# Cross-attention kernel: one unit of a batch's value projections moved from the fourth stretch of its half to the third

## The chip, the cores and the metric

The kernel runs on one core of a Trainium2 chip. The metric is the device time of one execution in microseconds; before the change the median of 3 runs is 1578.23 us (1575.32 to 1578.86).

## The reference, cut to what matters

`x` has 32 batches of 64 rows by 256; the context has 1601 rows by 256 for each batch. Three layers follow each other; the change lies in the first, cross-attention with 16 heads of 16.

```python
qh = _split_heads(q @ wq_w.T + wq_b)          # q = layernorm(x)
kh = _split_heads(k @ wk_w.T + wk_b)          # k = v = context
vh = _split_heads(v @ wv_w.T + wv_b)          # the values' projection
scores = jnp.einsum('bhqd,bhkd->bhqk', qh, kh) / jnp.sqrt(jnp.float32(D_K))
scores = jnp.where(mask, scores, jnp.float32(-1000000000.0))
attn = jax.nn.softmax(scores, axis=-1)
out = jnp.einsum('bhqk,bhkd->bhqd', attn, vh)
```

A second layer (a span attention, with `W_span`, `W_val`, `W_out`) works on the 64 rows of each batch, a third is a mixture of experts. All is float32.

## The kernel before, in words

**Halves.** The first layer goes through 64 halves, `n` = 0 to 63: half `n` is batch `b` = n // 2 and `c` = n % 2, eight of the sixteen heads. The context's 1601 rows are cut into 13 blocks of 124 (the last has 113), in four groups `GROUPS` of 4, 3, 3 and 3 blocks. Work is pipelined: in half `n` the scores of half `n + 1` are made, the exponentials of half `n`, the products with the values of half `n - 1`, and the projections of batch `b + 1`.

**Stretches.** A half runs through four stretches, `g` = 0 to 3, one for each group. In stretch `g`:

- `scores(n + 1, g, ...)`: PE multiplies queries and keys into four banks of PSUM (`psc`, L495), DVE adds the mask and puts them into `prob` (L504), and takes running maxima (`maximum`, L525). The last running maximum writes `mx`.
- `project_keys` for batch `b + 1`: PE makes `pk` (L450 by way of `product`), ACT copies it with its bias into `kT` (L465). In stretch 3 it is tiled.
- `project_values(b + 1, u, tiled)`: one unit `u` is two blocks of 124 rows (unit 6 has one), PE makes `pv` (L450), ACT copies it into `v` (L482). Untiled, a block takes two matmuls of 124 output rows; tiled, each is cut into four of 32 (the last of 28), at their own columns of the array. The profile counts two instructions for each float32 matmul, so a unit is 8 matmul instructions untiled and 32 tiled, each with a load of its weights.
- `less_maxima` on POOL (L556), an `exponentials` on ACT (L561), and one step of what the agenda holds for this stretch (`run`): steps of the queries of the next two batches (`query_steps`) and of the second layer for a pair of batches (`span_steps`), with work on all engines, such as `po` (L218, PE).

In stretch 0 the maxima of half `n` are also turned: `pm` (L532, PE) waits for `mx`, DVE reduces it to `mc` (L539), `pb` (L547, PE) spreads it, ACT copies it to `mb` (L551), and POOL takes it off. The products with the values, `values(n - 1, r)` (`pvs`, L571), stand in two parts: one ahead of stretch 0, one at its end.

**Order and banks.** PE, DVE, ACT and POOL run in the order in which the program is written (`manual_schedule`). All of `psc`, `pk`, `pv`, `pm`, `pb`, `po` and their like share the six banks of `ps_x`; a product waits until the bank that it is given has been read out.

**Where the units stand.** For batch `b + 1`, the first half (`c` = 0) makes unit 0 in stretch 1 and units 1 and 2, tiled, in stretch 3; the second half makes unit 3 in stretch 1, unit 4 in stretch 2, units 5 and 6, tiled, in stretch 3. Stretch 2 of a first half has none.

## Time and profile before

| | |
|---|---|
| median of 3 runs | 1578.23 us (1575.32 to 1578.86) |
| the profiled execution | 1579.34 us, its span 1577.4 us |
| mean granted clock of TensorE | 0.995 |
| `pv` untiled, 128*124 128x256 | 792 matmul instructions |
| `pv` tiled, 128*32 and 128*28 128x256 | 2604 and 744 matmul instructions |
| PE matmul and weight-load instructions | 28600 and 28600 |
| PE waits: `psc` L495 for DVE `prob` L504 (from 40 to 1390 us) | 20.9 us, 43 times |
| PE waits: `pm` L532 for DVE `mx` L525 (from 40 to 1390 us) | 4.6 us, 14 times |

The span is the time from the first instruction to the last. A line of a timeline gives the start of a run of like instructions, how long it lasts, the engine, the line of the kernel, the operation, output and inputs with their sizes (for PE rows*columns of the weights and the moving block), how many there are, and in brackets the idle time of the engine before it and what ended it. Ends of matmuls are modelled, so runs overlap their followers by some tenths of a microsecond, and start to start is the better measure. A line of the windows view gives a window's bounds and length, the busy time and count of PE, PEld, DVE, ACT and POOL, then the granted clock of TensorE, the DMA share and GB/s.

### The profile page before, as it was taken

Reading aid. Unit: us, or ns where it says so; the run is one execution under the profiler, and the core shown is the slowest. Engines: PE = TensorE matmul, PEld = TensorE weight load, DVE = VectorE, ACT = ScalarE, POOL = GpSimd, SP = SyncE. Lnnn points to the kernel's source line nnn. Section 1 sums busy time; section 2 is a strip of 40 time slices with the busy share of each in tenths; the row PEclk is TensorE's granted clock in tenths of the full one; section 3 lists DMA queues with packets and bytes.
Section 4 is the critical chain, followed back from the end, with each engine's and each line's share of the span. In section 5 each row is a group of like instructions: output and inputs, shape, how many; then the busy total and the mean of one; then the engine's idle time right before and its main releaser. Section 6 shows DMA issues by size and latency. Waiting matters only on the chain.

```text
span 1577.4 us, 62735 instructions
## 1 busy us (share of the span) xinstructions
PE 1518.3 (96%) x28600; PEld 1090.8 (69%) x28600; DVE 1259.5 (80%) x2700; ACT 897.1 (57%) x1229; POOL 1121.6 (71%) x424
## 2 busy tenths in 40 slices
PE   8999999999999999999999999999999999988899
PEld 5676776777767676676767676676767676754587
DVE  4888889898888888898889988898888988884200
ACT  2565656566565656656666656565655656555311
POOL 1777877878687877788786977788786878761610
PEclk9999999999999999999999999999999999999999
DMA  5111111111111111111111111111111111004100
GB/s 166 54 42 44 36 38 38 45 51 44 51 44 44 39 41 35 35 51 44 52 44 51 36 43 38 38 38 45 51 44 52 44 37 41 7 2 154 57 27 27
DMA packets 52072, 73.78 MB, mean 47 GB/s; under 512 B 3812, under 2 KB 51040, under 8 KB 51680
## 3 DMA queue, kind: packets, MB, share of 16 engines
q1 hardware_dynamic: 50992, 69.00, 15.3%
q8 instruction: 224, 3.67, 1.0%
q10 hardware_dynamic: 816, 0.79, 0.2%
q14 instruction: 40, 0.33, 0.1%
HBM read 65.57 MB, written 4.19 MB: 44 GB/s over the span
## 4 chain that ended last, share of the span: by engine, by line
PE 60%; DVE 36%; issue 2%; ACT 1%; DMA 1%; POOL 1%; ACTq 0%; SPq 0%; DVEq 0%; POOLq 0%
DVE prob L504 14%; PE pv L450 13%; PE pk L450 13%; DVE mrun L525 12%; PE pvs L571 9%; PE psc L495 9%; PE py L853 4%; PE u L600 3%; PE pm L532 2%; PE ph L835 2%; PE pb L547 1%; DVE total L313 1%; DVE least L308 1%; DVE mrun L293 1%; PE po L343 1%
## 5 line engine op out<-in xcount | busy, mean ns | idle before, releaser
L556 POOL TENSOR_TENSOR prob<-prob,mb 124x1664 f32<-124x1664 f32 x252 | 936.6, 3735 | 275.2 <-ACT mb L551 188.2
L504 DVE TENSOR_TENSOR prob<-psc,madd 124x384 f32<-124x384 f32 (+1 forms) x1024 | 567.5, 580 | 152.2 <-PE psc L495 152.2
L525 DVE TENSOR_TENSOR mrun<-prob,mrun 124x512 f32<-124x512 f32 x704 | 483.5, 687 | 3.9
L561 ACT ACTIVATE prob<-prob 124x1664 f32<-124x1664 f32 x256 | 403.1, 1587 | 26.0 <-POOL prob L556 23.0
L450 PE MATMUL pk<-ct,wkT_sb 128*32 128x361 f32 (+2 forms) x1768 | 404.8, 499 | 9.5 <-DMA wkT_sb<-in_wkT 5.4
L450 PE MATMUL pv<-wvT_sb,ct 128*32 128x256 f32 (+3 forms) x4268 | 385.8, 379 | 0.0
L450 PEld LDWEIGHTS pv<-wvT_sb,ct 128*32 128x32 f32 (+3 forms) x4268 | 258.6, 123 | 128.8 <-issue 16.3
L495 PE MATMUL psc<-qbd,kT 32*124 32x128 f32 x6656 | 288.2, 285 | 24.1 <-DVE prob L504 21.5
L465 ACT ACTIVATE kT<-pk,cols 128x372 f32<-128x372 f32 (+2 forms) x256 | 152.1, 594 | 239.4 <-PE pk L450 239.1
L495 PEld LDWEIGHTS psc<-qbd,kT 32*124 32x124 f32 x6656 | 226.2, 181 | 89.3 <-DVE prob L504 47.0
L482 ACT COPY v<-pv 124x512 f32<-124x512 f32 (+1 forms) x224 | 124.9, 558 | 211.0 <-PE pv L450 210.8
L450 PEld LDWEIGHTS pk<-ct,wkT_sb 128*32 128x32 f32 (+1 forms) x1768 | 158.6, 145 | 119.3 <-issue 51.5
L571 PE MATMUL pvs<-prob,v 124*17 124x64 f32 x13312 | 213.2, 220 | 2.3 <-issue 2.2
L571 PEld LDWEIGHTS pvs<-prob,v 124*17 124x17 f32 x13312 | 195.8, 98 | 22.5 <-issue 13.8
L517 ACT COPY mrun<-prob 124x512 f32<-124x512 f32 x64 | 38.5, 602 | 59.5 <-DVE soft L295 56.3
L855 DVE SCALAR_TENSOR_TENSOR ot<-py,prob 128x256 f32<-128x256 f32 x16 | 6.8, 425 | 75.7 <-PE py L853 66.1
L600 PE MATMUL u<-xfT,sw_sb 128*128 128x512 f32 x128 | 60.2, 620 | 1.3 <-ACT vbd L262 0.9
L547 PEld LDWEIGHTS pb<-cst,mc 128*124 128x124 f32 x256 | 29.2, 136 | 36.5 <-DVE mc L539 29.4
L532 PE MATMUL pm<-cst,mx 124*128 124x124 f32 x256 | 40.7, 282 | 8.3 <-DVE mx L525 8.2
L525 DVE TENSOR_TENSOR mx<-prob,mrun 124x512 f32<-124x512 f32 x64 | 43.9, 686 | 2.2
L842 ACT ACTIVATE hT<-ph,cols 128x256 f32<-128x256 f32 x32 | 13.4, 471 | 56.3 <-PE ph L835 56.3
L600 PEld LDWEIGHTS u<-xfT,sw_sb 128*128 128x128 f32 x128 | 24.5, 198 | 29.9 <-issue 25.3
(126 smaller groups left out, 1143.4 us busy)
## 6 DMA issues: line engine op xcount, KB each, us to landing
ct<-in_ctxT SPq DMA_DIRECT2D x64, 372.0 KB, 3.2
ct<-in_ctxT SPq DMA_DIRECT2D x32, 496.0 KB, 3.6
ct<-in_ctxT SPq DMA_DIRECT2D x32, 361.0 KB, 3.1
w<-in_w SPq DMA_DIRECT2D x16, 256.0 KB, 5.9
x<-in_x SPq DMA_DIRECT2D x16, 128.0 KB, 2.2
x_kept<-x SPq DMA_DIRECT2D x16, 128.0 KB, 2.8
prob<-x_kept SPq DMA_DIRECT2D x8, 256.0 KB, 5.4
out<-ot SPq DMA_DIRECT2D x16, 128.0 KB, 1.9
```

Of the source, the lines that this page charges most:

```text
L450: nc.tensor.matmul(out[at:end], lhsT=lhsT[:, at:end], rhs=rhs, start=start, stop=stop, **(dict(tile_position=(0, at)) if tiled else {}),)
L465: nc.scalar.activation(kTs[c][:, k0 : k0 + kn], ps[:, :kn], AF.Identity, bias=cols[:, B_K + c : B_K + c + 1])
L482: nc.scalar.copy(vs[b % 2][:kn, 2 * u : 2 * u + n, :, :DK], ps[:kn, : n * D].rearrange("p (n h d) -> p n h d", n=n, d=DK),)
L495: nc.tensor.matmul(ps[:CHUNK, k * P : (k + 1) * P], lhsT=kTs[c][32 * j : 32 * j + 32, at : at + CHUNK], rhs=qbd[b // 2][32 * j : 32 * j + ...
L504: nc.vector.tensor_tensor(pair_of(n, j)[:, c0 : c0 + nb, :].rearrange("p k (e q) -> p k e q", e=2), ps[:CHUNK, : nb * P].rearrange("p (k e ...
L525: nc.vector.tensor_tensor(dst, block_of(n, k), run, ALU.max)
L532: nc.tensor.transpose(ps[:, j * CHUNK : (j + 1) * CHUNK], m[:CHUNK, j, :], ident[:CHUNK, :CHUNK])
L556: engine.tensor_tensor(sj, sj, m[:CHUNK, j, None, :].to_broadcast([CHUNK, NKC, P]), ALU.subtract)
L561: nc.scalar.activation(pair_of(n, j), pair_of(n, j), AF.Exp)
L571: nc.tensor.matmul(pvs[32 * j : 32 * j + DK + 1, c, :, r, :], lhsT=v[:kn, k, 8 * c + h, :], rhs=pair_of(n, h // 2)[:kn, k, (h % 2) * S : ( ...
L600: nc.tensor.matmul(ps, lhsT=w[:, c, hc * P : (hc + 1) * P], rhs=xfT[:, c, :, slot], start=(c == 0), stop=(c == 1),)
L853: nc.tensor.matmul(py, lhsT=x, rhs=w, start=(n == 0), stop=(n == len(terms) - 1))
```

## The change

Unit 1 moves from stretch 3 to stretch 2 of a first half, and is no longer tiled. Stretch 3 of a first half keeps unit 2, tiled. Second halves are as they were. The loop makes batch `b + 1` in 31 first halves (`b` = 0 to 30); the units of batch 0 are made ahead of it and are not touched.

```diff
                 project(project_keys, c, g, g == 3)
                 if g == 1:
                     project(project_values, 3 * c)
-                elif g == 2 and c:
-                    project(project_values, 4)
-                elif g == 3:
-                    for u in range(5 if c else 1, 7 if c else 3):
+                elif g == 2:
+                    project(project_values, 3 * c + 1)
+                else:
+                    for u in (5, 6) if c else (2,):
                         project(project_values, u, True)
             if g:
                 less_maxima(n, g, m, nc.gpsimd)
```

On PE's queue the unit's matmuls now stand between the keys of stretch 2 and the agenda's step and scores that follow; on ACT's queue its copy stands ahead of the agenda's step and the exponential of stretch 2. No other engine's queue and no DMA changes its order.

## The prediction

> **What bounds the kernel now.** I read the page's busy shares and chain of waits first, then the timelines of PE and DVE over four halves in mid run, and last the busy time and granted clock of short windows.

> ```profile
> PE 1518.3 (96%) x28600; PEld 1090.8 (69%) x28600; DVE 1259.5 (80%) x2700; ACT 897.1 (57%) x1229; POOL 1121.6 (71%) x424
> PE 60%; DVE 36%; issue 2%; ACT 1%; DMA 1%; POOL 1%; ACTq 0%; SPq 0%; DVEq 0%; POOLq 0%
> ```

> PE and DVE take turns on the chain. I take the starts of pm (L532), one a half, as milestones. A half's usual length depends on its place in a cycle of two batches: A (even batch, first half) 21.96 us, B (even, second) 22.22, C (odd, first) 23.05, D (odd, second) 19.91; together 87.14. The change touches A and C. This is PE in one C (batch 13, from 601.53), from the keys of stretch 2 on:

> ```profile
> 612.99 1.52 PE L450 MATMUL pk<-ct,wkT_sb 128*128 128x372 f32 x4
> 614.44 0.97 PE L495 MATMUL psc<-qbd,kT 32*124 32x128 f32 x6
> 616.00 0.92 PE L495 MATMUL psc<-qbd,kT 32*124 32x128 f32 x18 [0.59 <-DVE prob L504]
> 616.84 1.42 PE L450 MATMUL pk<-ct,wkT_sb 128*32 128x361 f32 x16
> 618.08 3.64 PE L450 MATMUL pv<-wvT_sb,ct 128*32 128x256 f32 x64
> 621.53 1.64 PE L571 MATMUL pvs<-prob,v 124*17 124x64 f32 x104
> 623.10 1.15 PE L495 MATMUL psc<-qbd,kT 32*124 32x128 f32 x32
> 624.58 0.61 PE L532 MATMUL pm<-cst,mx 124*128 124x124 f32 x4 [0.33 <-DVE mx L525]
> ```

> The scores of stretch 3 stand from 614.44 to 616.84, 2.40 us for what takes 0.86 elsewhere (632.85 to 633.71): 1.54 us lost on a bank that DVE has not emptied. DVE is busy all through C and ends it:

> ```profile
> 617.52 1.01 DVE L504 TENSOR_TENSOR prob<-psc,madd 124x384 f32<-124x384 f32 x2
> 623.75 0.69 DVE L525 TENSOR_TENSOR mx<-prob,mrun 124x512 f32<-124x512 f32 x1
> ```

> mx ends at 624.44 and pm starts 0.14 us later. A is alike, with the scores at 569.00 to 570.85 (0.99 lost) and mx ending at 578.49:

> ```profile
> 569.00 0.48 PE L495 MATMUL psc<-qbd,kT 32*124 32x128 f32 x4
> 569.78 0.92 PE L495 MATMUL psc<-qbd,kT 32*124 32x128 f32 x20 [0.30 <-DVE prob L504]
> 577.55 1.15 PE L495 MATMUL psc<-qbd,kT 32*124 32x128 f32 x32
> 578.64 0.64 PE L532 MATMUL pm<-cst,mx 124*128 124x124 f32 x4
> ```

> So in A and C the end is DVE's. B and the start of D are PE's: in D, DVE stands 2.35 us until PE has done pm, pk, pb, pvs and the scores of stretch 1 (624.58 to 629.74).

> **The moved unit itself.** In 31 first halves unit 1 leaves stretch 3 and enters stretch 2. Tiled it cost half of 618.08 to 621.53, 1.73 us. Untiled, keys then unit then scores take 1.36 + 1.81 (633.71, 635.07, 636.88, in a D) against 1.45 for keys then scores (612.99 to 614.44): 1.72. Net 0.0. Each half issues 24 matmuls and 24 weight loads fewer; no DMA, POOL or SP work moves.

> **Is DVE made late?** In C the unit runs 614.35 to 616.17, while the scores would have waited. They start at 616.17, and D shows 0.95 from such a start to DVE's first read (628.81 to 629.76): 617.12, and DVE wants them at 617.52, so 0.4 us of cover. In A: unit, then po (0.96), scores at 570.73, readable at 571.68; wanted at 572.57. Cover 0.9. Banks: the unit takes the free bank, so the scores use those of stretch 2, as in D, where 24 scores run unbroken and only the tiled keys wait, 0.14. Without the cover: if the fourth score waited for DVE's last read of stretch 2 (616.46 + 0.54 = 617.00), 18 more instructions at 0.84 would end at 617.84 and DVE start near 618.0, 0.46 later in each of 14 C. That is the upper bound; below nothing it can't go, DVE being busy throughout.

> **ACT.** The unit's copy (L482) now stands ahead of L304 and L561 and waits for its matmuls (1.92 from their start, as 608.23 to 610.15): in C 616.27 instead of never. Behind it, the square ends near 617.8 (POOL wants it at 618.70) and the exponential near 619.3 (PE's pvs wants it at 620.0, being early itself). Nobody waits; 0.

> **Where PE's won time goes.** In C PE reaches the scores before pm at 616.17 + 0.86 + 1.24 + 1.73 + 1.57 = 621.57 and is done at 622.72. mx still ends at 624.44. So the losses of stretch 3 become one wait of **1.86 us** at pm. In A it is 0.9. Neither A nor C gets shorter. Three small gains:
> - Batches 0 and 1 are not DVE's at the end of their first half (pm 0.75 and 0.74 after mx, not 0.14): 0.6 each, 1.2.
> - PE's instruction supply. Queue q8 brings 3.67 MB in 224 packets, so 16.4 KB or 256 of PE's 57,200 instructions each, and PE sometimes stands until the next:

> ```profile
> q8 instruction: 224, 3.67, 1.0%
> 650.26 0.30 PE L571 MATMUL pvs<-prob,v 113*17 113x64 f32 x6 [0.62 <-issue]
> ```

> Nine A are longer than usual, by 4.75 us in all, and eight B, by 3.25. In four A (batches 8, 10, 20, 22) it falls in the last scores, 2.5 us: now inside the 0.9 us of wait. In B 2.8 of it falls soon after pm: packets asked for earlier, while PE waits at pm, come in time. All D, which follow a wait of 0.33 at pm, are 19.91 to 19.92 from batch 3 on. The early stalls of A (2.3) stay. Gain 5.3; bounds 0 and 8, as the 48 instructions shift where packets end.
> Sum: -1.2 - 5.3, about **-6 us**.

> **What the wait does to the clock.** This decides. Late in the run PE has gaps, and the granted clock falls to half for whole windows of 3.41 us on a fixed grid:

> ```profile
> 1389.46:1392.87 3.41, 1.88 (x40) 1.38 (x36) 2.79 (x6) 1.60 (x2) 0.00 (x0) 1.00 0.00 0
> 1427.01:1430.42 3.41, 1.38 (x100) 1.21 (x88) 3.20 (x8) 2.38 (x3) 1.89 (x1) 1.00 0.29 75
> 1430.42:1433.83 3.41, 3.34 (x12) 2.78 (x12) 0.65 (x2) 1.17 (x2) 0.02 (x1) 0.50 0.73 233
> 1464.55:1467.97 3.42, 1.60 (x29) 1.21 (x33) 0.66 (x1) 1.21 (x3) 1.47 (x1) 1.00 0.00 0
> ```

> The third number is PE's busy time, PEclk the third from the end. A window with 1.38 us busy (a gap of 2.10) is followed by 0.50, and so is 1.60; 1.88 is not (a gap of 1.53). The new gap, whole inside a window, leaves 3.41 - 1.86 = 1.55 busy: below one that fell. Cost: at half clock 104 pvs took 2.98 us (1416.20) against 1.64, so a window loses 3.41 / 2 = **1.7 us**, just after C's pm, where D is PE's and nothing hides it.

> How often: the window needs at least 3.41 - 1.60 = 1.81 of the gap. That holds for (3.41 + 1.86 - 3.62) / 3.41 = 48% of positions. A cycle of 87.14 is 25.53 windows, so after a kept C the next gap lies half a window on; with 1.7 lost it is 88.84, 26.03 windows, and the next falls again until leftover stalls carry it out. I estimate 11 of the 14 C from batch 3 on: **+18.7 us**. Bounds: 0 (threshold under 1.55 busy) and 14 x 1.7 = 24. I take near the upper one, as 1.55 is nearer to 1.60, which fell, than to 1.88. A's 0.9 us gap leaves 2.5 busy, above 1.88: no fall.

> [...]

> **Sum.** -6 + 18.7 = +12.7. On the profiled execution's 1579.34 (span 1577.4) that is 1592.0; it stands 1.1 over the median 1578.23, so **1591** as a median.

> **Rivals.** (1) The clock holds, as the threshold lies lower or the gap comes out under 1.6: only -6, 1572 (1569 to 1575). For: every C loses 1.54 us in one place today and keeps 1.00. Against: the 1.60 window. (2) It holds and supply stalls merely move: -1.2 or so, 1577 (1575 to 1581). (3) The scores starve DVE: the bank case above, 14 x 0.46 = +6.4, and -1.2: 1583. It decides once the scores are over 0.4 us late. Against: D's unbroken scores.

> **Chances.** Forecast 0.54, its own range 1584 to 1597; rivals 0.28, 0.12, 0.06. Range 1571 to 1596. A measurement here tells 0.2%, 3.2 us: faster 0.28, same 0.12, slower 0.54 + 0.06 = 0.60.

> **What would show it.** PE's wait at pm for mx grows to near 1.9 us in C and 0.9 in A, and the scores' waits for DVE fall from 20.9 us to near 9 (those of stretch 2). Windows after C's pm stand at 0.50 and D grows to 21.6; the mean clock falls from 0.995 to near 0.983. If D stays 19.91, the clock step is wrong; if C grows past 23.05, the cover of DVE is.

## The result, and the profile after

After the change a run takes 1578.22 us (median of 20, 1570.56 to 1588.58), before it 1578.84 (20 runs, 1575.32 to 1583.53). The ratio is 0.9996, with an interval from 0.9982 to 1.001: no change that can be told. The forecast was 1591. The profiled execution after took 1575.67 us, its span 1573.6.

PE's line, the chain and the instruction queue on the page of after:

```profile
PE 1499.1 (95%) x27856; PEld 1094.7 (70%) x27856; DVE 1258.5 (80%) x2700; ACT 895.6 (57%) x1229; POOL 1121.5 (71%) x424
PE 55%; DVE 41%; issue 2%; ACT 1%; POOL 1%; DMA 0%; DVEq 0%; ACTq 0%; POOLq 0%
q8 instruction: 218, 3.57, 0.9%
```

PE has 744 matmuls and as many weight loads fewer, which is 24 in each of 31 first halves. PE's share of the chain has gone from 60% to 55%, DVE's from 36% to 41%. This is PE in the same C (batch 13) as in the prediction, from the keys of stretch 2 on:

```profile
610.05 1.52 PE L450 MATMUL pk<-ct,wkT_sb 128*128 128x372 f32 x4
611.40 1.89 PE L450 MATMUL pv<-wvT_sb,ct 128*124 128x256 f32 x8
613.22 0.93 PE L495 MATMUL psc<-qbd,kT 32*124 32x128 f32 x24
614.12 1.42 PE L450 MATMUL pk<-ct,wkT_sb 128*32 128x361 f32 x16
615.36 1.91 PE L450 MATMUL pv<-wvT_sb,ct 128*32 128x256 f32 x32
617.09 1.64 PE L571 MATMUL pvs<-prob,v 124*17 124x64 f32 x104
618.65 1.15 PE L495 MATMUL psc<-qbd,kT 32*124 32x128 f32 x32
621.55 0.64 PE L532 MATMUL pm<-cst,mx 124*128 124x124 f32 x4 [1.74 <-DVE mx L525]
```

The scores of stretch 3 run unbroken (613.22 to 614.12, where it was 2.40 us), and all that PE won stands as one wait of 1.74 us at pm. PE's waits from 40 to 1390 us, in total, times and longest:

```profile
PE pm L532 <- DVE mx L525: 34.4, 28, 1.7
PE psc L495 <- DVE prob L504: 7.9, 14, 0.6
```

Before, these were 4.6 us in 14 and 20.9 us in 43. The wait has changed its place, as the prediction said. The halves from batch 3 on, 14 of each kind, summed from start of pm to start of pm:

| | before, us | after, us | usual one, before and after |
|---|---|---|---|
| A | 312.17 | 309.42 | 21.96, 21.95 |
| B | 314.32 | 313.52 | 22.22, 22.19 |
| C | 322.71 | 321.31 | 23.05, 22.97 |
| D | 278.79 | 281.06 | 19.91, 19.95 |

One D is 21.63 long (batch 23). It holds the only window at half clock in the loop of this execution, from 1057.83 on; such a window is called a fall below, and the window or gap ahead of it is said to have fallen. The forecast had eleven of these. Two windows of after on the grid of 3.41 us, and the one behind the second (bounds and length, busy time and count of PE, PEld, DVE, ACT and POOL, granted clock, DMA share and GB/s):

```profile
532.17:535.59 3.42, 1.68 (x26) 1.17 (x19) 3.35 (x7) 1.46 (x2) 3.42 (x2) 1.00 0.00 0
1054.41:1057.83 3.42, 1.68 (x64) 1.38 (x52) 3.35 (x6) 1.45 (x2) 3.42 (x2) 1.00 0.02 5
1057.83:1061.24 3.41, 3.41 (x8) 1.81 (x8) 2.73 (x5) 1.23 (x1) 1.47 (x1) 0.50 0.00 0
```

Both of the first two hold a whole gap of 1.74 or 1.75 us and 1.68 us of PE's busy time. The first was kept at full clock afterwards and the second was followed by a fall. So the measure by which the prediction counted does not separate the two.

**The whole time, over runs.** A run's time times its mean granted clock takes the loss at half clock out, as an estimate that counts each such window half; the clock is given to 0.001, or 1.6 us, so only means count. Before: 1573.4 (the mean of the 23 runs timed beside the first experiments; on the other chips 1572.3 to 1573.4), so 6.0 us lost, nearly all behind the loop (the profiled execution stands at half clock from 1413.35 and three more times, and not earlier). After: 1565.3, the mean of 20 runs, with 13.2 lost. So the change wins about 8 us and gives about 7 back to the clock, which is four windows a run at 1.7 us. The pair of profiles says the same with a smaller win: without their half-clock windows of 3.41 and 6.83 us, counted half, the spans are 1568.9 and 1563.4, so -5.5. The profiled execution of before is the one that stands off: the spans of the 23 runs, reckoned with their clocks, have a mean of 1571.4.

### The profile page after: what moved, and what is told of

Its sections match the earlier page's. It is cut to its first block, busy times and chain, and to the rows that moved or that the text cites. A ratio compares the mean times of both kernels' runs of the same rounds, so it can differ in the third digit from the quotient of the medians.

```text
span 1573.6 us, 61215 instructions
## 1 busy us (share of the span) xinstructions
PE 1499.1 (95%) x27856; PEld 1094.7 (70%) x27856; DVE 1258.5 (80%) x2700; ACT 895.6 (57%) x1229; POOL 1121.5 (71%) x424
## 4 chain that ended last, share of the span: by engine, by line
PE 55%; DVE 41%; issue 2%; ACT 1%; POOL 1%; DMA 0%; DVEq 0%; ACTq 0%; POOLq 0%
DVE mrun L525 15%; DVE prob L504 15%; PE pk L450 13%; PE pv L450 11%; PE psc L495 8%; PE pvs L571 8%; PE py L853 4%; PE u L600 3%; PE pm L532 2%; PE ph L835 2%; PE pb L547 1%; DVE mx L525 1%; DVE total L313 1%; DVE least L308 1%; DVE mrun L293 1%
## 5 line engine op out<-in xcount | busy, mean ns | idle before, releaser
L504 DVE TENSOR_TENSOR prob<-psc,madd 124x384 f32<-124x384 f32 (+1 forms) x1024 | 568.6, 581 | 146.1 <-PE psc L495 146.1
L525 DVE TENSOR_TENSOR mrun<-prob,mrun 124x512 f32<-124x512 f32 x704 | 483.7, 687 | 3.9
L561 ACT ACTIVATE prob<-prob 124x1664 f32<-124x1664 f32 x256 | 403.3, 1588 | 46.7 <-POOL prob L556 43.7
L450 PE MATMUL pk<-ct,wkT_sb 128*32 128x361 f32 (+2 forms) x1768 | 406.0, 499 | 8.0 <-DMA wkT_sb<-in_wkT 5.4
L450 PE MATMUL pv<-wvT_sb,ct 128*124 128x256 f32 x3524 | 390.9, 379 | 0.0
L450 PEld LDWEIGHTS pv<-wvT_sb,ct 128*124 128x124 f32 x3524 | 273.5, 132 | 119.8 <-issue 16.8
L495 PE MATMUL psc<-qbd,kT 32*124 32x128 f32 x6656 | 267.9, 284 | 12.1 <-DVE prob L504 8.5
L495 PEld LDWEIGHTS psc<-qbd,kT 32*124 32x124 f32 x6656 | 214.3, 181 | 65.6 <-DVE prob L504 26.4
L450 PEld LDWEIGHTS pk<-ct,wkT_sb 128*32 128x32 f32 (+1 forms) x1768 | 159.0, 145 | 117.8 <-issue 53.1
L482 ACT COPY v<-pv 124x512 f32<-124x512 f32 (+1 forms) x224 | 124.8, 557 | 202.6 <-PE pv L450 202.4
L571 PE MATMUL pvs<-prob,v 124*17 124x64 f32 x13312 | 212.5, 220 | 1.1 <-issue 0.9
L571 PEld LDWEIGHTS pvs<-prob,v 124*17 124x17 f32 x13312 | 195.7, 98 | 21.1 <-issue 10.8
L532 PE MATMUL pm<-cst,mx 124*128 124x124 f32 x256 | 41.1, 284 | 38.5 <-DVE mx L525 38.0
L532 PEld LDWEIGHTS pm<-cst,mx 124*128 124x128 f32 x256 | 26.8, 142 | 48.4 <-DVE mx L525 29.6
L525 DVE TENSOR_TENSOR mx<-prob,mrun 124x512 f32<-124x512 f32 x64 | 43.9, 686 | 2.2
```

What stands on the lines that cost most here:

```text
L450: nc.tensor.matmul(out[at:end], lhsT=lhsT[:, at:end], rhs=rhs, start=start, stop=stop, **(dict(tile_position=(0, at)) if tiled else {}),)
L482: nc.scalar.copy(vs[b % 2][:kn, 2 * u : 2 * u + n, :, :DK], ps[:kn, : n * D].rearrange("p (n h d) -> p n h d", n=n, d=DK),)
L495: nc.tensor.matmul(ps[:CHUNK, k * P : (k + 1) * P], lhsT=kTs[c][32 * j : 32 * j + 32, at : at + CHUNK], rhs=qbd[b // 2][32 * j : 32 * j + ...
L504: nc.vector.tensor_tensor(pair_of(n, j)[:, c0 : c0 + nb, :].rearrange("p k (e q) -> p k e q", e=2), ps[:CHUNK, : nb * P].rearrange("p (k e ...
L525: nc.vector.tensor_tensor(dst, block_of(n, k), run, ALU.max)
L532: nc.tensor.transpose(ps[:, j * CHUNK : (j + 1) * CHUNK], m[:CHUNK, j, :], ident[:CHUNK, :CHUNK])
```

## The experiments

All are timed against the kernel before on the same chip, and the ratio is to that. From chip to chip the median of the kernel before goes from 1576.33 to 1579.9, so medians of different rows compare to some 3 us only. "Lost" is the mean loss at half clock worked out as above; the kernel before loses 4.6 to 6.8 us by chip, so some 6 us of it is not the change's.

| kernel | median us | ratio, interval | gap at pm in C | falls in the profiled loop | lost, us |
|---|---|---|---|---|---|
| the change | 1578.22 | 0.9996 (0.9982 to 1.001) | 1.74 | 1 | 13.2 |
| moved in A alone | 1571.44 | 0.9945 (0.9926 to 0.9964) | as before | 0 | 5.5 |
| moved in C alone | 1583.62 | 1.0028 (1.0012 to 1.0044) | 1.74 | 1 | 12.3 |
| gap filled | 1576.96 | 0.9978 (0.9966 to 0.9991) | 0.78 | 0 | 5.9 |
| moved unit still tiled | 1571.09 | 0.9949 (0.9937 to 0.9961) | 1.64 | 0 | 4.7 |
| one tile's instructions out | 1575.63 | 0.9994 (0.9974 to 1.0014) | 1.75 | 2 | 13.3 |
| a quarter of a term out | 1578.85 | 1.0014 (0.9996 to 1.0033) | 1.85 | 4 | 14.6 |
| half of a term out | 1591.69 | 1.0095 (1.008 to 1.011) | 1.96 | 12 | 26.3 |
| a whole term out | 1590.15 | 1.0074 (1.0056 to 1.0093) | 2.18 | 12 | 24.4 |
| unit 2 out | 1591.96 | 1.0076 (1.006 to 1.0091) | 2.52 | 12 | 27.3 |
| keys of D ahead of pm | 1570.64 | 0.9938 (0.9925 to 0.9952) | filled | 0 | 6.8 |
| and the maxima earlier | 1566.31 | 0.9919 (0.9901 to 0.9937) | filled | 0 | 6.8 |
| both without the move | 1587.99 | 1.0066 (1.0046 to 1.0087) | none | 0 | 5.3 |

**The change in A alone, and in C alone.** Two theories stand against each other: the clock takes in C what the move wins (the forecast's, with fewer falls), or the move wins nothing.

```diff
-                elif g == 2:
+                elif g == 2 and (c or b % 2 == 0):
                     project(project_values, 3 * c + 1)
-                else:
-                    for u in (5, 6) if c else (2,):
+                elif g == 3:
+                    for u in (5, 6) if c else (2,) if b % 2 == 0 else (1, 2):
```

> Unit 1 is moved in even batches' first halves (A) only; odd ones (C) are as before the change. Theory 1 (the clock: the move saves some 5 us by hiding PE's supply stalls in a wait at pm, and half-clock windows after C's pm take it back, about three a run at 1.7 us): no long wait in C, so no fall there; mean clock near 0.995, time 1573 to 1576 where before is 1578.8. Theory 2 (supply stalls only move, and the clock plays no part): within 2 us of before.

> Unit 1 is moved in odd batches' first halves (C) only. Theory 1: the falls stay and the gain in A is missing, clock 0.988 to 0.993, time 1578 to 1584, slower than e1_even by 4 us or more. Theory 2: within 2 us of before and of e1_even.

In C alone the two conditions are `b % 2` in place of `b % 2 == 0`. In A alone gives 1571.44, under what was expected; in C alone 1583.62. Without the loss, A alone stands at 1565.8 and C alone at 1571.4, against 1573.4 before. So most of the win is A's (7.6 against 2.0), and the loss comes with the move in C.

**The gap filled.** One matmul ahead of pm in D whose product nobody reads:

```diff
+                    if c and b % 2:
+                        ps = mm_bank("fill")
+                        nc.tensor.matmul(ps, lhsT=ident, rhs=sw1[:, 0, :], start=True, stop=True)
```

> The change, and ahead of pm in odd batches' second halves (D) one 128x512 product of constants that nobody reads (0.86 us of PE), so that the wait there is partly filled. It adds PE work and nothing useful. Theory 1: no half-clock window before the last 180 us, clock 0.994 or more in every run, D always 19.95, time 1571 to 1575, below the change by 3 us or more. Theory 2: as the change or slower.

The gap shrank to 0.78, no window fell in the profiled loop, and over 12 runs the loss is 5.9, as in the kernel before (6.0 on that chip). So the gap is what the clock answered to: with it at 1.74 a run of the change loses 13.2. The time missed what was expected by 2 us: the mean without loss is 1570.7, 5.4 over the change. C is 23.06 and D 20.07, 0.2 more a cycle than in the change, so filling costs nearly 3 us in 14 cycles; the rest is not accounted for.

**The moved unit still tiled.** In the change the unit is also made untiled; here it moves and stays tiled.

```diff
-                    project(project_values, 3 * c + 1)
+                    project(project_values, 3 * c + 1, c == 0)
```

> The change, but the moved unit stays tiled (32 matmul instructions, as before the change) in its new place. Theory 1: what counts is the place and not the tiling, so C 22.97, a wait of 1.7 us at pm, a few falls, mean clock 0.988 to 0.994 and a time within 4 us of the change (1575 to 1583). Rival 3 (the gain of the change comes from 1488 fewer instructions on PE's supply): the supply stalls of before come back, some 5 us, and the time is 1582 or more.

It missed, on the good side: 1571.09. The reason is in PE's timeline of a C:

```profile
621.23 0.64 PE L532 MATMUL pm<-cst,mx 124*128 124x124 f32 x4 [1.64 <-DVE mx L525]
```

The gap is 1.64, a tenth less than in the change, and no window falls. From the keys of stretch 2 to the last scores PE takes 8.70 us here (609.73 to 618.43) and 8.60 in the change (610.05 to 618.65), so the tiled unit is a tenth longer in its new place, and that tenth comes off the gap. Without the loss the time stands at 1567.1, only 1.8 over the change: the place of the unit makes most of the win, and the fewer instructions little. Untiling it won some 1.8 us and cost some 8.5 of clock (4.7 lost here, 13.2 in the change).

**How long a gap may be.** Five kernels of the change with less work on PE in C's stretch 3 ask this. They leave a part of the values' projection out, so that the gap at pm widens; their results are of no use otherwise. Unit 2 out in odd batches:

```diff
-                    for u in (5, 6) if c else (2,):
+                    for u in (5, 6) if c else () if b % 2 else (2,):
```

> The change, with unit 2 of the values of batches 2, 4, ... 30 left out (made in odd batches' first halves, C), so PE does 1.73 us less in each C and its wait at pm grows from 1.74 to about 3.4 us. Theory 1: the clock falls after nearly every C, 13 or 14 of 14, D grows by 1.7 us or more each, clock 0.98 or less, time 1594 to 1605 in spite of less work. Theory 2: less PE work, so the time of the change or less.

The second contraction term of unit 2's second block out:

```diff
-            for i in range(2):
+            terms = 1 if short and n else 2
+            for i in range(terms):
...
-                        project(project_values, u, True)
+                        project(project_values, u, True, not c and b % 2)
```

> The change, and of unit 2 in odd batches' first halves (C) the second block's second term of the contraction is left out (0.43 us less of PE in each C), so the wait at pm grows from 1.74 to about 2.17 us. Theory 1, with the threshold where the two traces put it (a 3.41 us window falls when PE streams for 0.37 of it or less and stays at 0.41 or more): a gap of 2.17 lies under it wherever it is inside one window by some 2.05 us, so falls lock on as in e6_longgap and 8 to 13 of 14 D are longer by 1.6 us: 1584 to 1593, clock 0.983 to 0.989. If the threshold is elsewhere or the falls have another cause: as the change, 1574 to 1581.

Both show what the forecast had described, at larger gaps: 12 falls each, most of them 88.75 us apart; with unit 2 out each D with a fall takes 21.3 to 21.6. Unit 2 out missed its own figures on the low side: its gap is 2.52 and not 3.4, for PE now also stands 0.76 us ahead of the values' products, where ACT's exponential (L561) is not out, and it falls 12 times and not 13 or 14. Then the size that the prediction had worked out, 1.86:

```diff
...
         for at in range(0, n, 32) if tiled else (0,):
+            if short and at == 96 and stop: continue
...
```

> Change, but in odd first halves (C) the second block of unit 2 goes without the second contraction term of its last 28 rows (two instructions, about 0.11 us; this leaves part of the values' projection out). PE's wait at pm in C should be 1.83 to 1.87 us, the size that the prediction had. Theory 1 (the count of falls was wrong mainly because the gap came out at 1.74, near the edge, and not at 1.86): 7 to 11 falls of the clock in the loop, granted clock 0.983 to 0.988, 1584 to 1592 us. Theory 2 (the prediction's threshold, from modelled busy time, was itself wrong, and 1.86 is no more harmful than 1.74): 0 to 5 falls, clock 0.989 to 0.996, 1573 to 1581 us.

This did not reach its gap: 1.75. With one of the four tiles of a term out, PE still takes 1.73 us from the unit's start to the values' products (613.52 to 615.25), as in the change (615.36 to 617.09). As an experiment on 1.86 it tells nothing. The gap is the change's, and so is the ratio (0.9994 and 0.9996). The next two cut columns in all four tiles (64, then 128), and there the same stretch takes 1.62 and 1.51:

```diff
-                    ps[:kn, n * D : (n + 1) * D], cts[b][g][:, i, k0 : k0 + kn], wvT[:, i, :],
+                    ps[:kn, n * D : (n + 1) * D - cut * i * n], cts[b][g][:, i, k0 : k0 + kn], wvT[:, i, : D - cut * i * n],
...
-                        project(project_values, u, True)
+                        project(project_values, u, True, 0 if c or b % 2 == 0 else 64)
```

> Change, but in odd first halves the second block of unit 2 gets its second contraction term in 192 of 256 columns only (this leaves part of the values' projection out). Cutting the whole term widened the gap at pm from 1.74 to 2.18, so a quarter should make it about 1.85, the size that the prediction had. Theory 1 (the count of falls was wrong mainly because the gap came out at 1.74, near an edge, and not at 1.86): 7 to 11 falls of the clock in the loop, granted clock 0.983 to 0.988, 1584 to 1592 us. Theory 2 (the prediction's threshold, from modelled busy time, was itself wrong, and 1.86 is hardly more harmful than 1.74): 1 to 5 falls, clock 0.989 to 0.996, 1573 to 1581 us.

> As the run before, with 128 of 256 columns: gap about 1.96. Both theories: more falls than at 1.85, no more than the 11 at 2.18. Theory 1: 9 to 11, clock 0.982 to 0.986, 1586 to 1592 us. Theory 2, the edge lying between 1.86 and 2.18: 4 to 8 falls, clock 0.986 to 0.991, 1579 to 1586 us.

At 1.85, 4 falls and 1578.85 us: theory 2. At 1.96, 12 falls and 1591.69: theory 1's time for the second run, with a fall more than it allowed; theory 2 had 4 to 8 falls there. So the edge lies between, and it is sharp. Two windows of the kernel with a gap of 1.85:

```profile
1056.49:1059.90 3.41, 1.56 (x37) 1.37 (x38) 3.34 (x6) 1.35 (x2) 3.41 (x2) 1.00 0.02 5
1059.90:1063.31 3.41, 3.41 (x7) 1.33 (x6) 2.42 (x5) 0.90 (x1) 1.13 (x1) 0.50 0.00 0
...
882.41:885.82 3.41, 1.56 (x37) 1.28 (x30) 3.34 (x6) 1.35 (x2) 3.41 (x2) 1.00 0.00 0
```

With 1.56 us busy, almost the prediction's 1.55, the first was followed by 0.50; the last was not. What differs to the eye is where the gap begins. Over the profiled executions, for gaps that lie whole in a window of the grid, by their start in it:

| gap | kept, start in the window | fell, start in the window |
|---|---|---|
| 1.64 | all 7, 0.02 to 1.72 | none |
| 1.74 to 1.75 (three kernels) | 15, 0.23 to 1.07 | 4, 1.45 to 1.59 |
| 1.85 | 4, 0.24 to 0.94 | 4, 1.04 to 1.54 |
| 1.96 | none | 10, 0.36 to 1.31 |
| 2.18 | none | 11, 0.43 to 1.11 |

No gap of 1.64 to 1.85 that straddled two windows felled one; two of 1.96 and one of 2.18 did. A late gap has pvs and psc in front of it, an early one has pm and pk of 496 columns behind it. That PE's work of the one kind counts for less is my guess, which no run shows by itself. I also worked out how long columns stream in each window, from 4 x 496 columns in the 1.67 us between pk and pb (622.03 to 623.70 in after), with overlapping instructions taken together: by that, in after and in the three kernels with gaps of 1.75, 1.85 and 1.96, windows of the loop with a share of 0.37 or less fell and those of 0.40 or more were kept, and between them 0.39 went both ways. Of the late windows of before in the prediction, the two that fell stand at 0.35 and 0.36 and the one that was kept at 0.42. An edge by this measure, between 0.37 and 0.41, stands in the expectation of the run with 2.18, ahead of that kernel and of those with 1.75, 1.85 and 1.96, and they fit it. No run tested the measure by itself.

**The keys of D ahead of pm.** If the gap is idle time of PE, work that D needs anyway can go there. pk of stretch 0 needs nothing of pm:

```diff
+                    if c and b % 2:
+                        project(project_keys, c, 0)
...
-                project(project_keys, c, 0)
+                if not (c and b % 2):
+                    project(project_keys, c, 0)
```

> The change, and in odd batches' second halves (D) the keys of stretch 0 (pk, 1.67 us) stand ahead of pm instead of behind it, so that the wait there is filled with work that has to be done. Theory 1 (the clock): no fall after C's pm, mean clock 0.994 to 0.997, no D with 1.7 us added; and D itself shorter by 0.3 to 0.5 us, as pk no longer stands between pm and pb. Time 1564 to 1571. Theory 2 (the time won by the move was never there): 1576 or more.

It came as expected, 1570.64. PE at the end of a C, by its timeline:

```profile
620.39 1.93 PE L450 MATMUL pk<-ct,wkT_sb 128*128 128x496 f32 x4
622.30 0.61 PE L532 MATMUL pm<-cst,mx 124*128 124x124 f32 x4
623.98 0.65 PE L547 MATMUL pb<-cst,mc 128*124 128x128 f32 x4 [1.07 <-DVE mc L539]
```

The wait at pm is gone, but pb now waits 1.07 us for mc, which DVE takes behind two evictions of scores (its copies of them out of PSUM, L504). D is 19.53, C 23.05.

**The maxima earlier too.** In D, mc goes behind the first eviction of scores:

```diff
-            if j == 1 and held is not None:
+            if j == after and held is not None:
...
-                scores(n + 1, g, BETWEEN[g], turn)
+                scores(n + 1, g, BETWEEN[g], turn, 0 if c and b % 2 else 1)
```

> Change plus pk of stretch 0 ahead of pm in D, plus the mask's maxima mc on VectorE after the first score block of stretch 0 instead of the second. Theory 1 (what is left in D is the wait for mc ahead of pb, 1.07 us): mc ends one eviction (about 0.65 us) earlier, the wait ahead of pb becomes about 0.45, D 18.9 to 19.2 (from 19.53), no fall of the clock in the loop, granted clock 0.994 to 0.998, 1560 to 1567 us. Rival (the second score block's eviction, put off behind mc, holds up pm's product or the next use of its bank): D as in the run before at 19.5, 1568 to 1573 us.

```profile
618.06 1.93 PE L450 MATMUL pk<-ct,wkT_sb 128*128 128x496 f32 x4
619.97 0.61 PE L532 MATMUL pm<-cst,mx 124*128 124x124 f32 x4
621.35 0.65 PE L547 MATMUL pb<-cst,mc 128*124 128x128 f32 x4 [0.77 <-DVE mc L539]
```

D is 19.23 and the median 1566.31, the best of all. The wait ahead of pb is 0.77 and not 0.45, because mc is now held by pm itself (DVE waits 0.20 us for it).

**Both edits without the move.** The kernel before with these two edits:

> The kernel before (unit 1 tiled in stretch 3) with the two edits in D alone: pk of stretch 0 ahead of pm, and mc after the first score block. It tells what the move of the unit is worth when no gap falls. Theory 1 (the move wins 6 to 8 us by itself): D as 19.2 to 19.4, 1571 to 1575 us, against 1566 with the move. Rival (the move is worth nothing, and the gain of the last two runs is all from the two edits in D): 1565 to 1569 us.

Both expectations missed by far: 1587.99. PE in the same C, and DVE's mc:

```profile
626.84 1.15 PE L495 MATMUL psc<-qbd,kT 32*124 32x128 f32 x32
627.92 1.93 PE L450 MATMUL pk<-ct,wkT_sb 128*128 128x496 f32 x4
629.69 0.59 PE L532 MATMUL pm<-cst,mx 124*128 124x124 f32 x4
```

```profile
627.49 0.69 DVE L525 TENSOR_TENSOR mx<-prob,mrun 124x512 f32<-124x512 f32 x1
...
630.32 0.67 DVE L539 TENSOR_REDUCE mc<-pm 128x4 f32<-128x496 f32 x1 [1.54 <-PE pm L532]
```

mx is out at 628.18, but PE is still at pk until 629.69, and DVE then stands 1.54 us. A usual C is 24.42 and the fourteen take 343.11, 20.4 more than before; D wins 10.0 of that back (268.78). The sum, +10.4, is the difference of the medians within 0.1 (1577.47 to 1587.99 on that chip). I had not seen that without the move there is no gap to fill. So the gap that cost the change its win is also the room that the best version lives on.

## Why the prediction was wrong

**The step that failed** is in "What the wait does to the clock": "the window needs at least 3.41 - 1.60 = 1.81 of the gap", and from it 11 falls and +18.7 us. The price of a fall was right (D 21.63 in place of 19.95, 1.68). The place was right (behind C's pm), the grid and the return after 26 windows too: at 1.96 and 2.18 us they come as described. The number was not: about 4 a run, and the term of +18.7 us measured +7. The reason is the threshold. It came from two late windows, 1.60 busy that fell and 1.88 that was kept, read as if busy time by the profile's model were what counts. Windows with 1.68 did both in after, and at 1.85, a hundredth under the size forecast, 1.56 did both too. The gap's own size was a smaller error: 1.74, not 1.86. By the rule as written, 1.74 would have felled none, so neither size gives the 4 that came. A gap of 1.86 would have made some 5 or 6 falls a run, (14.6 - 6.0) / 1.7 or, with what the kernel before lost on that chip, (14.6 - 4.6) / 1.7, and no slower kernel, as the 1578.85 us at 1.85 (ratio 1.0014, 0.9996 to 1.0033) show. The forecast would have held from 1.96 on, a tenth of a microsecond more. The runs put the edge between gaps of 1.64, where none of 7 fell, and 1.96, where all 10 that lay whole in a window did.

**The moved unit** cost nothing net on PE (from the keys of stretch 2 to the end of the last scores 9.75 us, where 9.73 were forecast), and the scores of stretch 3 came in time: C got no longer, so the third rival (scores starve DVE) falls. C is even 0.08 shorter, which the prediction excluded: pm starts 0.05 after mx is out (DVE's timeline has it from 620.81 for 0.69, to 621.50; pm follows at 621.55) where it was 0.14. These 0.09 are also most of what the gap came out short. D gives 0.04 of it back.

**The small gains.** Batches 0 and 1 won 0.3 each and not 0.6 (18.50 to 18.20 and 20.65 to 20.35). Of the supply stalls A won 2.75, where 2.5 were forecast, B 0.8 and not 2.8, and C 1.4, most of it the 0.08 above. In sum -5.5 in the profiles and -8 over runs, for -6. So the second rival (supply stalls merely move) falls as well: a good half of the win in the loop is A's. The stalls were hidden rather than removed: PE's idle time for which the profile shows no cause ("issue") is 3.4 us before and 3.7 after, from 40 to 1390 us, and of A's waits at pm, usually 0.8, three are 0.3 to 0.6. That these stalls are the supply of instructions was argued from the packets, and no run tests it by itself. The profiles show that 1488 instructions fewer are 6 packets fewer (224 to 218), 248 each, and that all 8 such stalls before stand at the same place of 256, counted over PE's instructions in order (the 7 after within three places). But with the unit tiled, and so with the old number of instructions, most of the win was there.

**The first rival** (the clock holds, 1572) had the right sum for everything but the clock, and is what happens at 1.64 (1571.09). The true case lay between it and the forecast, and I gave no chance to a threshold that catches some gaps and not others.

## What to carry to other kernels

Small waits that are only gathered into one cost nothing by the engines and can still cost the clock: four windows of 3.41 us took back all that this change had won. When a change leaves one long gap on PE, look for work behind it that does not depend on what PE waits for, and put it in the gap; that made of a change worth nothing one worth 0.8%, and without the gap the same edits cost 0.7%. A threshold read from two windows is a bound for windows with that mix of work, not a rule, and a forecast built on it should carry the case in between.
